# The third step of a graph layer: eight batches' operands stay in SBUF, the bias goes to TensorE, the power moves by a turn

## The chip, the core and the metric

One Trainium2 chip, and of it one core. The metric is the device time of one execution in microseconds; the kernel before has a median of 3002.88 us over three runs (3001.03 to 3012.99).

## The reference, cut to what matters

Four graph layers run over 16 batches of 1024 nodes with 128 features and a dense 0/1 adjacency; each adds its result to its input and normalises. The change is in layer 1, a GraphSAGE of three steps with a batch norm after each:

```python
def _sage(x, adj, Wr, Wx, b, mf):
    deg = jnp.clip(jnp.sum(adj, axis=-1, keepdims=True), 1.0, None)
    agg = jnp.einsum('bij,bjd->bid', adj, x) / deg
    out = agg @ Wr + x @ Wx + b
    nrm = jnp.maximum(jnp.linalg.norm(out, axis=-1, keepdims=True), NORM_EPS)
    return out / nrm * mf[..., None]

h1 = _bn(relu(_sage(x,  adj_d, Wr1, Wx1, b1, mf)), g1, be1)
h2 = _bn(relu(_sage(h1, adj_d, Wr2, Wx2, b2, mf)), g2, be2)
h3 = _bn(relu(_sage(h2, adj_d, Wr3, Wx3, b3, mf)), g3, be3)
out = concat([h1, h2, h3]) @ Wl + bl
```

The batch norm takes mean and variance over all batches and nodes, so no step can begin its products before the step ahead of it has ended its statistics for all 16 batches. The same holds for layer 2, which needs h3.

## The kernel before, in words

`adj_d` is a thinned adjacency that a stage before layer 1 makes. It lies in SBUF as 8-bit numbers, 8 KB per partition and batch: `Y[8]` to `Y[15]` stay where they were made (the left `carry` pool), while `Y[0]` to `Y[7]` are stored to DRAM and loaded again, batch by batch, in steps one and two.

A `Step` has four parts for each batch, each a generator that yields between stages. `load` brings in h transposed (`hT`) and the aggregate (`ag`), 512 KB each, on SP's queue. `out` makes x Wx + agg Wr in two PSUM banks of four node blocks each (L1405), adds the bias row on VectorE (L1407), squares on ScalarE into PSUM (L1413), sums on VectorE (L1414), raises to -1/2 on GpSimd (L743 on VectorE and L744 on GpSimd, inside `power_mhalf`), multiplies by the mask (L1417), and writes n = relu(o) times that factor (L1421). `keep` transposes n (TensorE, L758), copies it to `nT` (ScalarE, L1430), takes the statistics (VectorE, L1431) and stores nT to DRAM from GpSimd's queue (L1432), as the next step and layer 2 read it. In the first two steps `keep` also makes the aggregate for the next step: it splits n in two parts (L1267, L1268), widens the 8-bit adjacency (L1288, L1290), multiplies (L1301), scales by the degree (L1440) and stores `ag` (L1442, GpSimd's queue). The third step has no aggregate to make.

`norm` and `take_norm` close a step: the statistics are combined (L1335), GpSimd raises to -1/2 again, and the batch norm's scale and shift are folded into the next step's weights and bias row (L1328 to L1331).

The order of the turns is written by hand in the loop at the end: all steps go through batches 8 to 15 and then 0 to 7, with loads one or two turns ahead. In the third step a turn holds the first stage of `out` of its batch, the remaining stages of `out` of the batch before, and `keep` of the batch before that. `take_turns` goes round the streams, one stage of each. The order on each engine comes from that source order, and from a planner that moves an instruction forward when it expects the earlier ones to have to wait: the first products of layer 2 (L1563) stand among the last turns of the third step. Each engine executes its own list in order.

Buffers that matter: ps_h and ps_a are two pools of four PSUM banks each. In the third step ps_h serves both the products of `out` and the transposes of `keep`, and ps_a is idle but for the last aggregate of step two. `o` has two buffers, `nT` two, `n`, `ag` and the h of the third step three each.

Of the kernel before, what the change touches and what calls it, by code (L numbers as in the profile page):

```python
# [22 lines left out]
P = 128  # L23
# [616 lines left out]
def fast_kernel(ctx: ExitStack, tc: tile.TileContext, t: dict, out: bass.AP, flag: bass.AP):  # L640
# [612 lines left out]
    with ExitStack() as ph:  # L1253
# [39 lines left out]
        def adjacency_product(pieces, parts):  # L1293

            for h in range(H2):
# [6 lines left out]
                                             start=(jt == 0 and p == 0), stop=(jt == NT - 1 and p == 1))  # L1302
                yield acc, slice(h * 512, (h + 1) * 512)

        class Step:


# [14 lines left out]
            def take_norm(self):  # L1322

                ab = bn_ab[self.l - 1]
                ws = wts.tile([P, P], F32, name="ws")
                nc.vector.tensor_add(ws, self.Wr, self.Wx)
                pc = ps_h.tile([P, P], F32, name="pc", tag="h")
                nc.tensor.matmul(pc, ab[:, 1:2].to_broadcast([P, P]), ws, start=True, stop=True)  # L1328
                nc.vector.tensor_add(self.brow, self.brow, pc)
                nc.vector.tensor_scalar(self.Wr, self.Wr, ab[:, 0:1], None, op0=OP.mult)  # L1330
                nc.vector.tensor_scalar(self.Wx, self.Wx, ab[:, 0:1], None, op0=OP.mult)  # L1331

            def norm(self):
                mv = wts.tile([P, 2], F32, name=f"bmv{self.l}")
# [7 lines left out]
            def load(self, b):  # L1342
                st = self.batches[b]
                if self.l < 2:
                    st.A = Y[b]
                    if b < B // 2:
                        st.A = wide_pool.tile([P, NT, N], FP8, name="A8", bufs=4)
                        nc.sync.dma_start(st.A.bitcast(F32), dil8_d[b])
                if self.l == 0:
                    st.x = work.tile([P, NT, P], F32, name="n", bufs=3)  # L1350
                    nc.sync.dma_start(st.x, nat(x1_d[b]))
                else:

                    tag, bufs = ("rdeg", 3) if self.l == 2 else ("hT", 2)
                    st.hT = work.tile([P, N], F32, name="hT", tag=tag, bufs=bufs)
                    nc.sync.dma_start(st.hT, hT_d[self.l - 1][b])
                    st.ag = work.tile([P, N], F32, name="ag", bufs=3)
                    nc.sync.dma_start(st.ag, ag_d[b])
                    if self.l < 2:
                        self.load_rdeg(b)  # L1360
                yield
# [34 lines left out]
            def out(self, b):  # L1396

                st = self.batches[b]
                o = work.tile([P, NT, P], F32, name="o", tag="oT")
                banks = []  # L1400
                for p, _, blocks in halves(ps_h):
                    banks.append(tiles3(p))
                    for i, j in enumerate(blocks):
                        for n, (x, W) in enumerate(((st.hT, self.Wx), (st.ag, self.Wr))):
                            nc.tensor.matmul(p[:, i * P:(i + 1) * P], x[:, j * P:(j + 1) * P], W,  # L1405
                                             start=(n == 0), stop=(n == 1))
                    nc.vector.tensor_add(o[:, blocks[0]:blocks[-1] + 1, :], tiles3(p),  # L1407
                                         self.brow[:, None, :].to_broadcast([P, 4, P]))
                yield
                ss = small.tile([P, NT], F32, name="ss")  # L1410
                for h, sq in enumerate(banks):
                    k = slice(4 * h, 4 * h + 4)
                    nc.scalar.activation(sq, o[:, k, :], AF.Square)  # L1413
                    nc.vector.tensor_reduce(ss[:, k], sq, AX.X, OP.add)  # L1414
                yield
                rn = power_mhalf(small, ss, floor=1e-24, name="rn")
                nc.vector.tensor_mul(rn, rn, mf[:, b * NT:(b + 1) * NT])  # L1417
                st.n = work.tile([P, NT, P], F32, name="n", bufs=3)
                for h in range(H2):
                    k = slice(4 * h, 4 * h + 4)  # L1420
                    nc.vector.scalar_tensor_tensor(st.n[:, k, :], o[:, k, :], 0.0, half_rows(rn[:, k]),  # L1421
                                                   op0=OP.max, op1=OP.mult)
                yield

            def keep(self, b):

                st = self.batches[b]
                nT = work.tile([P, N], F32, name="nT", tag="hi" if self.l == 2 else "oT")
                for p, c, k in turned(ps_h, st.n):
                    nc.scalar.copy(nT[:, c], p)  # L1430
                    nc.vector.bn_stats(self.stats[:, b * H2 + k.start // 4, :], nT[:, c])  # L1431
# [2 lines left out]
                if self.l < 2:  # L1434
                    parts = split(st.n)
                    pieces = list(widened(st.A))
                    yield
                    ag = work.tile([P, N], F32, name="ag", bufs=3)
                    for acc, c in adjacency_product(pieces, parts):
                        nc.vector.tensor_mul(ag[:, c], acc, st.rdeg[:, c])  # L1440
                        yield
                    nc.gpsimd.dma_start(ag_d[b], ag)  # L1442
                yield

        before = None
# [5 lines left out]
        for l in range(3):  # L1451
            step = Step(l, before)
            if l:
                before.norm()
                step.take_norm()
            lead = 0 if l == 1 else 1
            take_turns([step.load(b) for b in order[:1 + lead]])
            if l == 0:
# [2 lines left out]
            for i in range(B + lag[l]):  # L1461
# [3 lines left out]
                if l == 0 and i + 1 < B:  # L1465
                    streams.append(step.first(order[i + 1]))
                if i < B:
                    streams.append(outs[i] if l < 2 else islice(outs[i], 1))
                if l == 2 and i:
                    streams.append(outs[i - 1])  # L1470
                if i > lag[l]:
# [277 lines left out]
```

## Time and profile before

| what | value |
|---|---|
| median of 3 runs | 3002.88 us (3001.03 to 3012.99) |
| span of the profiled execution, first to last instruction | 2999.4 us |
| PE busy, whole span | 2738.3 us (91%) |
| VectorE (DVE) busy | 2327.9 us (78%) |
| ScalarE (ACT) busy | 2028.5 us (68%) |
| GpSimd (POOL) busy | 324.1 us (11%) |
| mean DMA rate over the span | 99 GB/s |
| layer 1, second step | about 1535 to 1717 us |
| layer 1, third step | 1717.1 us (first product) to 1825.1 us (last statistics) |

The profile comes from a single execution. Its time as a whole is not listed beside the span; the median of the runs is 3.5 us above the span, and that difference is what lies around the first and the last instruction. Busy times are sums of instruction durations with overlapping ones counted once; VectorE's instructions of 128x512 elements last 0.68 us but start every 0.60 us, since each begins before the one ahead of it has drained. PE rows with "x2" show two instructions of one matmul in fp32, which is executed in two passes.

### The profile page before, as it was taken

Reading aid. Unit: us, or ns where it says so; the run is one execution under the profiler, and the core shown is the slowest. Engines: PE = TensorE matmul, PEld = TensorE weight load, DVE = VectorE, ACT = ScalarE, POOL = GpSimd, SP = SyncE. Lnnn points to the kernel's source line nnn. Section 1 sums busy time; section 2 is a strip of 40 time slices with the busy share of each in tenths; the row PEclk is TensorE's granted clock in tenths of the full one; section 3 lists DMA queues with packets and bytes.
Section 4 is the critical chain, followed back from the end, with each engine's and each line's share of the span. In section 5 each row is a group of like instructions: output and inputs, shape, how many; then the busy total and the mean of one; then the engine's idle time right before and its main releaser. Section 6 shows DMA issues by size and latency. Waiting matters only on the chain.

```text
span 2999.4 us, 43064 instructions
## 1 busy us (share of the span) xinstructions
PE 2738.3 (91%) x15282; PEld 1714.8 (57%) x15282; DVE 2327.9 (78%) x5990; ACT 2028.5 (68%) x3476; POOL 324.1 (11%) x295
## 2 busy tenths in 40 slices
PE   7999999996999998999999988999999999999996
PEld 3444444443566566887788874455555555555554
DVE  6898888887999995776688885766767777777765
ACT  5777787784788877666555534766766776666763
POOL 0000000003000001111122231000010001000000
PEclk9999999998999999999999997999999999999998
DMA  4344344431000024223367692111111121111000
GB/s 157 134 162 148 134 147 155 141 134 43 2 2 2 2 82 163 86 99 129 128 238 241 234 342 98 36 57 57 64 70 57 65 70 69 57 56 57 22 15 23
DMA packets 124129, 297.98 MB, mean 99 GB/s; under 512 B 12672, under 2 KB 65664, under 8 KB 116736
## 3 DMA queue, kind: packets, MB, share of 16 engines
q1 hardware_dynamic: 103440, 211.65, 20.8%
q0 software_dynamic: 20464, 83.47, 7.4%
q8 instruction: 123, 2.02, 0.3%
q14 instruction: 102, 0.84, 0.1%
HBM read 211.04 MB, written 84.02 MB: 98 GB/s over the span
## 4 chain that ended last, share of the span: by engine, by line
PE 36%; DVE 23%; issue 21%; ACT 8%; DMA 6%; POOL 5%; SPq 0%; POOLq 0%; ACTq 0%; DVEq 0%
PE ph L1545 8%; PE acc L1301 7%; PE ph L765 4%; PE acc L1621 4%; DMA an<-in_adj 4%; POOL ln_rstd L744 3%; PE pmm L723 3%; DVE ln_st L793 3%; PE ph L1405 3%; ACT xn L800 3%; PE ph L758 3%; DVE em L1607 2%; PE ph L1531 2%; ACT em L969 2%; PE acc L976 2%
## 5 line engine op out<-in xcount | busy, mean ns | idle before, releaser
L723 PE MATMUL pmm<-G,hT 128*128 128x512 f32 x1024 | 503.1, 608 | 7.6 <-DVE mx L1607 7.2
L800 ACT ACTIVATE xn<-xn,ln_nb,ln_rstd 128x128 f32<-128x128 f32 x512 | 207.3, 481 | 108.7 <-DVE ln_nb L798 108.7
L723 PEld LDWEIGHTS pmm<-G,hT 128*128 128x128 f32 x1024 | 178.2, 192 | 175.5 <-issue 140.6
L976 PE MATMUL acc<-em,hs 128*128 128x512 f32 x512 | 243.5, 598 | 16.6 <-DVE hs L973 15.0
L1301 PE MATMUL acc<-a,lo 128*128 128x512 f32 x768 | 243.4, 401 | 15.7 <-DVE lo L1268 15.7
L744 POOL TENSOR_TENSOR ln_rstd<-ln_rstd,mhalf 128x8 f32<-128x8 f32 (+1 forms) x68 | 113.6, 1671 | 1320.0 <-DVE nmx L1609 603.7
L1621 PE MATMUL acc<-em,hs 128*128 128x512 f32 x512 | 249.7, 606 | 3.5 <-DVE hs L1618 1.9
L1301 PE MATMUL acc<-a,hi 128*128 128x512 f32 x768 | 244.0, 402 | 3.7 <-ACT hi L1267 3.5
L1138 PE MATMUL s<-step,carry 128*128 128x512 bf16 (+2 forms) x1088 | 211.6, 307 | 4.1 <-DVE carry L1108 3.2
L1140 ACT ACTIVATE q<-s,negc 128x512 f16<-128x512 f32 x256 | 170.6, 697 | 58.4 <-DVE negc L1119 22.3
L922 ACT ACTIVATE ab<-an 128x1024 bf16<-128x1024 f32 x128 | 134.6, 1053 | 106.2 <-DMA an<-in_adj 79.5
L1152 ACT ACTIVATE carry<-pc,negone 128x512 fp8e4<-128x512 f32 x256 | 166.8, 699 | 37.0 <-PE pc L1151 27.7
L965 DVE CUSTOM_DVE_ANT_0 em<-pmm,msk 128x1024 f32<-128x1024 f32 x128 | 155.9, 1218 | 30.4 <-PE acc L976 26.5
L1607 DVE CUSTOM_DVE_ANT_0 em<-pmm,msk 128x1024 f32<-128x1024 f32 x128 | 155.6, 1216 | 26.1 <-PE acc L1621 21.3
L1301 PEld LDWEIGHTS acc<-a,lo 128*128 128x128 f32 x768 | 144.2, 190 | 54.9 <-DVE lo L1268 21.3
L925 DVE SCALAR_TENSOR_TENSOR chk<-an 128x1024 fp8e4<-128x1024 f32 x128 | 156.3, 1221 | 15.5 <-DMA an<-in_adj 15.4
L1301 PEld LDWEIGHTS acc<-a,hi 128*128 128x128 f32 x768 | 143.0, 190 | 37.1 <-ACT hi L1267 4.0
L1602 ACT ACTIVATE msk<-A,nbig 128x1024 bf16<-128x1024 fp8e4 x128 | 145.8, 1140 | 26.6 <-DVE mx L1607 23.4
L930 DVE TENSOR_SCALAR carry<-pt 128x1024 fp8e4<-128x1024 bf16 x128 | 155.5, 1216 | 7.0 <-PE pt L929 6.9
L976 PEld LDWEIGHTS acc<-em,hs 128*128 128x128 f32 x512 | 90.6, 190 | 113.0 <-issue 87.9
L969 ACT ACTIVATE em<-em,nmx 128x1024 f32<-128x1024 f32 x128 | 146.8, 1147 | 11.9 <-DVE nmx L967 11.5
L1405 PE MATMUL ph<-Wx,hT 128*128 128x128 f32 x768 | 151.6, 280 | 3.0 <-ACT nT L1430 1.5
(293 smaller groups left out, 6252.8 us busy)
## 6 DMA issues: line engine op xcount, KB each, us to landing
an<-in_adj SPq DMA_DIRECT2D x128, 512.0 KB, 4.1
adj_d<-carry POOLq DMA_DIRECT2D x16, 1024.0 KB, 4.9
A<-dil_d SPq DMA_DIRECT2D x16, 1024.0 KB, 6.8
rdeg<-rdeg_d SPq DMA_DIRECT2D x32, 512.0 KB, 4.1
ag_d<-ag POOLq DMA_DIRECT2D x32, 512.0 KB, 5.3
ag<-ag_d SPq DMA_DIRECT2D x32, 512.0 KB, 6.1
A<-adj_d SPq DMA_DIRECT2D x16, 1024.0 KB, 4.7
xn<-in_x SPq DMA_DIRECT2D x16, 512.0 KB, 3.9
```

The lines of the kernel that those rows point to most:

```text
L723: nc.tensor.matmul(p[:, h * 512:(h + 1) * 512], lhsT, rhs[:, h * 512:(h + 1) * 512], start=True, stop=True)
L744: nc.gpsimd.tensor_tensor(r, r, mhalf[:, :n], op=OP.pow)
L800: nc.scalar.activation(r[:, k.start + i, :], r[:, k.start + i, :], AF.Identity, scale=rstd[:, i:i + 1], bias=nb[:, i:i + 1])
L969: nc.scalar.activation(em, em, AF.Exp, bias=nmx, accum_out=sm)
L976: nc.tensor.matmul(s.acc[:, c], hs, em[:, c], start=(jt == 0), stop=(jt == NT - 1))
L1138: nc.tensor.matmul(s[:, lo or 0:], y, twos if lo is None else step[:, :512 - lo], start=(j == 0), stop=(j == len(terms) - 1))
L1140: nc.scalar.activation(q[:, h * 512:(h + 1) * 512], s, AF.Abs, bias=st.negc[:, i:i + 1])
L1301: nc.tensor.matmul(acc, part[:, jt, :], pieces[h * NT // 2 + i][:, j, :], start=(jt == 0 and p == 0), stop=(jt == NT - 1 and p == 1))
L1405: nc.tensor.matmul(p[:, i * P:(i + 1) * P], x[:, j * P:(j + 1) * P], W, start=(n == 0), stop=(n == 1))
L1545: nc.tensor.matmul(p, part[:, jt, :], A[:, jt, c], start=(jt == 0 and i == 0), stop=(jt == NT - 1 and i == 1))
L1607: nc.vector.tensor_tensor_reduce(em, e, msk, 1.0, 0.0, op0=OP.add, op1=OP.max, accum_out=mx)
L1621: nc.tensor.matmul(s.acc[:, c], hs, em[:, c], start=(jt == 0), stop=(jt == NT - 1))
```

## The change

Three parts, all for the third step (`l == 2`).

Where h and the aggregate live. When the second step reaches batch b of 0 to 7, the adjacency `Y[b + 8]` has had its last use eight turns before. `home(b)` takes that memory, 8 KB per partition, as two fp32 rows of 1024: the first becomes nT of batch b, the second its aggregate. The third step's `load` then hands over these two and issues no DMA. nT is still stored to DRAM, because layer 2 reads it; ag of these batches is not. The order of the third step alternates the two kinds of batches: 8, 0, 9, 1, and so on to 15, 7.

The bias. Each bank of the third step's `out` is opened by a bf16 product of 512 columns: a matrix of twos against `bias3`, which holds half the bias row in three bf16 parts in rows 0, 32 and 64 and zeros elsewhere. The products of h and ag accumulate on it. The results stay in PSUM, now in ps_a; the square reads it there and writes `o` in SBUF, and n reads it there. `split_bias` makes the three parts on VectorE at the step's start.

The power. In the third step the second stage of `out` (squares, sums) now also issues the power, and the loop runs two stages of `out` in its batch's own turn; the multiplication by the mask and n come in the turn after.

```diff
--- before.py
+++ after.py
@@ -1302,6 +1302,11 @@
                                              start=(jt == 0 and p == 0), stop=(jt == NT - 1 and p == 1))
                 yield acc, slice(h * 512, (h + 1) * 512)
 
+        def home(b):
+
+            words = Y[b + B // 2].bitcast(F32).rearrange("p t n -> p (t n)")
+            return words[:, :N], words[:, N:]
+
         class Step:
 
 
@@ -1329,6 +1334,21 @@
                 nc.vector.tensor_add(self.brow, self.brow, pc)
                 nc.vector.tensor_scalar(self.Wr, self.Wr, ab[:, 0:1], None, op0=OP.mult)
                 nc.vector.tensor_scalar(self.Wx, self.Wx, ab[:, 0:1], None, op0=OP.mult)
+                if self.l == 2:
+                    self.split_bias()
+
+            def split_bias(self):
+
+                self.bias3 = wts.tile([P, P], BF16, name="bias3")
+                nc.vector.memset(self.bias3, 0.0)
+                rest = wts.tile([P, P], F32, name="ws")
+                nc.vector.tensor_scalar(rest, self.brow, 0.5, None, op0=OP.mult)
+                for i in range(3):
+                    part = wts.tile([P, P], BF16, name="part")
+                    nc.vector.tensor_copy(part, rest)
+                    nc.vector.tensor_copy(self.bias3[32 * i:32 * i + 1, :], part[32 * i:32 * i + 1, :])
+                    if i < 2:
+                        nc.vector.tensor_sub(rest, rest, part)
 
             def norm(self):
                 mv = wts.tile([P, 2], F32, name=f"bmv{self.l}")
@@ -1349,6 +1369,8 @@
                 if self.l == 0:
                     st.x = work.tile([P, NT, P], F32, name="n", bufs=3)
                     nc.sync.dma_start(st.x, nat(x1_d[b]))
+                elif hasattr(st, "home"):
+                    st.hT, st.ag = st.home
                 else:
 
                     tag, bufs = ("rdeg", 3) if self.l == 2 else ("hT", 2)
@@ -1397,35 +1419,48 @@
 
                 st = self.batches[b]
                 o = work.tile([P, NT, P], F32, name="o", tag="oT")
+                end = self.l == 2
                 banks = []
-                for p, _, blocks in halves(ps_h):
+                for p, _, blocks in halves(ps_a, "acc") if end else halves(ps_h):
                     banks.append(tiles3(p))
+                    if end:
+                        nc.tensor.matmul(tiles3(p), twos[:, :P], self.bias3[:, None, :].to_broadcast([P, 4, P]),
+                                         start=True, stop=False)
                     for i, j in enumerate(blocks):
                         for n, (x, W) in enumerate(((st.hT, self.Wx), (st.ag, self.Wr))):
                             nc.tensor.matmul(p[:, i * P:(i + 1) * P], x[:, j * P:(j + 1) * P], W,
-                                             start=(n == 0), stop=(n == 1))
-                    nc.vector.tensor_add(o[:, blocks[0]:blocks[-1] + 1, :], tiles3(p),
-                                         self.brow[:, None, :].to_broadcast([P, 4, P]))
+                                             start=(n == 0 and not end), stop=(n == 1 and (i == 3 or not end)))
+                    if not end:
+                        nc.vector.tensor_add(o[:, blocks[0]:blocks[-1] + 1, :], tiles3(p),
+                                             self.brow[:, None, :].to_broadcast([P, 4, P]))
                 yield
                 ss = small.tile([P, NT], F32, name="ss")
-                for h, sq in enumerate(banks):
+                for h, bank in enumerate(banks):
                     k = slice(4 * h, 4 * h + 4)
-                    nc.scalar.activation(sq, o[:, k, :], AF.Square)
+                    x, sq = (bank, o[:, k, :]) if end else (o[:, k, :], bank)
+                    nc.scalar.activation(sq, x, AF.Square)
                     nc.vector.tensor_reduce(ss[:, k], sq, AX.X, OP.add)
+                if end:
+                    rn = power_mhalf(small, ss, floor=1e-24, name="rn")
                 yield
-                rn = power_mhalf(small, ss, floor=1e-24, name="rn")
+                if not end:
+                    rn = power_mhalf(small, ss, floor=1e-24, name="rn")
                 nc.vector.tensor_mul(rn, rn, mf[:, b * NT:(b + 1) * NT])
                 st.n = work.tile([P, NT, P], F32, name="n", bufs=3)
                 for h in range(H2):
                     k = slice(4 * h, 4 * h + 4)
-                    nc.vector.scalar_tensor_tensor(st.n[:, k, :], o[:, k, :], 0.0, half_rows(rn[:, k]),
+                    nc.vector.scalar_tensor_tensor(st.n[:, k, :], banks[h] if end else o[:, k, :], 0.0, half_rows(rn[:, k]),
                                                    op0=OP.max, op1=OP.mult)
                 yield
 
             def keep(self, b):
 
                 st = self.batches[b]
-                nT = work.tile([P, N], F32, name="nT", tag="hi" if self.l == 2 else "oT")
+                if self.l == 1 and b < B // 2:
+                    st.home = home(b)
+                    nT = st.home[0]
+                else:
+                    nT = work.tile([P, N], F32, name="nT", tag="hi" if self.l == 2 else "oT")
                 for p, c, k in turned(ps_h, st.n):
                     nc.scalar.copy(nT[:, c], p)
                     nc.vector.bn_stats(self.stats[:, b * H2 + k.start // 4, :], nT[:, c])
@@ -1435,11 +1470,13 @@
                     parts = split(st.n)
                     pieces = list(widened(st.A))
                     yield
-                    ag = work.tile([P, N], F32, name="ag", bufs=3)
+                    kept = hasattr(st, "home")
+                    ag = st.home[1] if kept else work.tile([P, N], F32, name="ag", bufs=3)
                     for acc, c in adjacency_product(pieces, parts):
                         nc.vector.tensor_mul(ag[:, c], acc, st.rdeg[:, c])
                         yield
-                    nc.gpsimd.dma_start(ag_d[b], ag)
+                    if not kept:
+                        nc.gpsimd.dma_start(ag_d[b], ag)
                 yield
 
         before = None
@@ -1453,6 +1490,8 @@
             if l:
                 before.norm()
                 step.take_norm()
+            if l == 2:
+                order = [b for pair in zip(order[:B // 2], order[B // 2:]) for b in pair]
             lead = 0 if l == 1 else 1
             take_turns([step.load(b) for b in order[:1 + lead]])
             if l == 0:
@@ -1465,7 +1504,7 @@
                 if l == 0 and i + 1 < B:
                     streams.append(step.first(order[i + 1]))
                 if i < B:
-                    streams.append(outs[i] if l < 2 else islice(outs[i], 1))
+                    streams.append(outs[i] if l < 2 else islice(outs[i], 2))
                 if l == 2 and i:
                     streams.append(outs[i - 1])
                 if i > lag[l]:
```

## The prediction

> **What bounds the kernel now.** I looked first at the busy times of all engines by stretch, to find the third step and its limit. It begins when the new weights are ready (first L1405 of the step at 1717.1 us) and its last statistics end at 1825.1 us: 108 us, 3.6% of the span of 2999.4 us. Nothing that the change touches outside it is late, so this is where it must be priced. Columns: stretch, length, then PE, weight load, DVE, ACT, POOL busy (instructions), granted PE clock, DMA share, GB/s.
>
> ```profile
> 1625.00:1717.00 92.00, 89.95 (x535) 77.70 (x534) 76.63 (x134) 52.64 (x68) 21.24 (x24) 1.00 0.73 251
> 1717.00:1733.00 16.00, 15.43 (x121) 14.51 (x121) 9.85 (x24) 3.43 (x7) 3.12 (x3) 1.00 0.60 186
> 1733.00:1745.00 12.00, 10.06 (x81) 9.21 (x82) 11.05 (x22) 4.22 (x9) 5.09 (x5) 1.00 0.98 354
> 1745.00:1760.00 15.00, 13.94 (x117) 12.85 (x116) 13.78 (x28) 5.61 (x12) 5.11 (x6) 1.00 0.91 310
> 1760.00:1775.00 15.00, 13.73 (x112) 12.47 (x113) 12.99 (x26) 6.52 (x12) 6.20 (x6) 1.00 0.98 382
> 1775.00:1790.00 15.00, 12.56 (x93) 10.36 (x91) 11.77 (x25) 4.29 (x8) 5.25 (x6) 1.00 1.02 388
> 1790.00:1805.00 15.00, 12.16 (x78) 10.22 (x76) 11.48 (x24) 4.28 (x8) 4.79 (x5) 0.89 1.03 379
> 1805.00:1812.00 7.00, 6.91 (x56) 6.08 (x55) 5.67 (x11) 2.20 (x4) 2.31 (x3) 1.00 0.36 142
> 1812.00:1822.00 10.00, 4.28 (x24) 2.47 (x23) 6.95 (x15) 3.19 (x6) 3.99 (x4) 0.91 0.62 212
> 1822.00:1850.00 28.00, 18.91 (x53) 10.70 (x51) 14.11 (x61) 14.37 (x30) 5.20 (x6) 0.56 0.21 75
> ```
>
> The first row is the second step: PE is busy 98% of it, so 4 MB fewer stores there buy nothing. In the third step three resources are nearly full at once: DMA (share 0.91 to 1.03 from 1733 to 1805), DVE (about 90% in the steady part), and PE. From 1717 to 1812 (the last product L1405) PE's busy times add to 84.8 of 95 us. **Only 10.2 us of PE idleness lie in the loop.** That sum decides the forecast.
>
> Next the order of time on DVE, steady part:
>
> ```profile
> 1759.81 1.28 DVE L1407 TENSOR_TENSOR o<-ph,b 128x512 f32<-128x512 f32 x2
> 1761.01 1.27 DVE L1431 BATCH_NORM_STATS2 stats<-nT 128x6 f32<-128x512 f32 x2
> 1762.20 0.15 DVE L743 TENSOR_SCALAR rn<-ss 128x8 f32<-128x8 f32 x1
> 1762.26 0.68 DVE L1414 TENSOR_REDUCE ss<-ph 128x4 f32<-128x512 f32 x1
> 1764.14 0.17 DVE L1417 TENSOR_TENSOR rn<-rn,mf 128x8 f32<-128x8 f32 x1 [1.19 <-POOL rn L744]
> ```
>
> A 128x512 instruction starts every 0.60 us. A turn has eight (L1407, L1414, L1421, L1431, two each), 4.8 us, and small ones; the wait for GpSimd's power adds 1.19 us every second turn. The chain of waits confirms DVE there, and names a store that held a buffer while DMA was full, and a load that PE waited for:
>
> ```profile
> 1733.87 10.22 DMA h2T_d<-nT
> ...
> 1764.30 0.60 DVE ss L1414
> 1764.90 0.61 DVE n L1421
> ...
> 1772.61 7.58 DMA hb<-h1T_d
> ```
>
> Last, PE at the end of the step:
>
> ```profile
> 1812.88 1.02 PE L1563 MATMUL py<-hb,Wl 128*128 128x512 f32 x2
> 1814.28 1.23 PE L758 MATMUL ph<-identf,n 128*128 128x128 f32 x8 [0.38 <-DVE n L1421]
> 1815.35 1.02 PE L1563 MATMUL py<-hb,Wl 128*128 128x512 f32 x2
> 1821.71 1.97 PE L758 MATMUL ph<-identf,n 128*128 128x128 f32 x8 [5.34 <-DVE n L1421]
> ```
>
> From the last L1405 (1812.0) to the end of the statistics it takes 13.1 us, most of it a serial chain through DVE, ACT and POOL; nothing of layer 2's real work can start before.
>
> [...] after 5.34 us of idling the eight transposes take 1.97 us instead of about 1.04, and the clock is 0.56 from 1822 to 1850. [...] in this trace bf16 and fp8 products of 512 columns follow each other in 0.22 to 0.31 us (L1138, L1148 at 902.7 to 903.7). [...]
>
> **The change part by part.**
>
> Bias to TensorE. Removed: 32 L1407 on DVE, 32 x 0.60 = 19.2 us of its issue time, and one link (0.69 us) of each batch's chain. Added: 32 bf16 products of 512 columns on PE. No row shows this operation with this neighbour (the f32 products around it), so bounds: 32 x 0.22 = 7.0 and 32 x 0.31 = 9.9 us; I take 0.25 each, **8.0 us**, on PE and not hidden, since PE will be the fullest engine. DVE falls to 6 x 0.60 + about 0.2 = 3.8 us a turn. PE's turn is 32 L1405 instructions at 0.111 us (3.57), eight transposes (0.88), about 0.1 for the change between them, plus 0.5: 5.05 us. The bound passes from DVE and DMA to PE.
>
> ACT's square now reads PSUM and writes SBUF, the reduction reads SBUF and n reads PSUM: 0.60, 0.68 and 0.68 us today with the sides the other way round, statistics from SBUF 0.68; taken as unchanged, ±0.05 us a turn and under cover of PE.
>
> Banks. A result now stays in one of four ps_a banks until L1421 has read it: two products' halves (4.5) then square 0.6, sum 0.6, L743 0.15, power 1.66 with about 0.25 of hand-over, L1417 0.17, two n 1.2: n is finished some 5.0 us after the batch's last product. PE has 0.88 + 4.5 + 0.88 = 6.3 us of other work before it needs that bank again. Hidden, with 1.3 us to spare; transposes keep ps_h alone, so the waits of L1405 for copies out of ps_h (ACT nT, and l2WT 1.30 at 1795.7) go.
>
> GpSimd a turn ahead. In the source L743 and the power close turn i, L1417 opens the work of turn i+1. Behind L1417 on DVE stand two n, and behind them PE's transposes. The two statistics of an older batch (1.2 us) and PE-paced gaps cover the 1.9 us. The 1.19 us waits go, but they were DVE's, no longer the bound: worth nothing beyond what is counted as idle below.
>
> Memory. For eight batches h, ag loads (16 issues on SP, 8.4 MB) and ag stores (8 on POOL at 0.58 us, 4.2 MB, in step two) go; h is still stored for layer 2. The step moves 300 GB/s x 109 us = 32.7 MB; less 8.4 and about 1 MB of late stores it is some 23 MB, under 260 GB/s in 92 us. DMA is no longer full. The 10.2 us store wait, and at least part of the 2.2 us that PE waited for hb, go. Alternating resident and loaded batches spreads the loads; nothing is added to SP's or POOL's queues. The home was last read eight turns before it is written: no wait.
>
> Split of the bias. DVE gains about ten small instructions after L1329: dependent 128x128 ones take 0.28 + 0.03 us (Wx L1331), six of them 1.9, row copies about 0.3: 2.2 us before the first product of the step can open its bank. 3.4 us of the last adjacency product (L1301, run at 1720.6) are ready to fill PE; if they go first the cost is 0, else 2.2. I take 1.0.
>
> Sum for the loop: busy 84.8, less 1.6 us lost to slow clock at 1796 to 1799 [...], plus 8.0, plus idle that remains, 3 of 10.2 (between 0 and 7): 94.2 against 95.0, **-0.8**. Start **+1.0**. Tail: from last product 0.65 (square), 0.65, 0.2, power 1.9, 0.2, n, transpose, copy, statistics of the last half 3.5: 7.1 against 13.1, **-6.0**, because L1407 no longer queues behind the preceding batch's wait for the power. [...] **-2** (0 to -8). Total -7.8. Against the profiled span that is 2991.6 us; the median of the runs shown, 3002.88, lies 3.5 above the span, so **2995 us**.
>
> **Rivals.** (1) Faster: PE packs tightly. Idle 1, bias 0.22: the loop is 84.8 - 1.6 + 7.0 + 1 = 91.2, -3.8; start 0; tail -6.5; and the clock holds after 1822, where 18.9 us of busy PE at 0.56 hide some 8 us, 6 on the chain: -16, **2987**. For it: DMA and DVE really are relieved. [...] (2) Slower: the power is not ahead. If DVE's queue has L1417 directly after its L743 (as at 1797, 1804, 1818: 1.79 us idle each) or n behind the next batch's sums, banks come back late and PE waits. Today's turn is (95.0 - 3.4 - 5.2 of L1563)/16 = 5.4 us; to lose 15 us over the 6 of the tail it has to be 6.7. Product 4.5, a late chain of 2.2 and no cover is that: 16 x 1.4 - 6 = +16, **3019**. Against: DVE has over 1 us a turn to spare. (3) Nothing comes through: start 2.2, bias 9.9, idle 6, tail -5: about +2, 3005. Layer 2's first work is placed among these turns by a plan made beforehand (L1563 runs at 1775, inside step three), so a new order can move a few us either way in any case.
>
> **How the numbers follow.** 0.5%, 15 us, is about what a measurement of this kernel can tell from no change. Forecast and rival 3 both lie within it: 0.68. Rival 1 and its neighbours beyond 15 us: 0.23. Rival 2: 0.09. The range 2982 to 3009 reaches past rival 1 and rival 3 and leaves out rival 2.
>
> **What would show it.** Right: no L1407 rows in step three, 32 bf16 products of 0.22 to 0.31 us spacing; DMA share under 0.8 from the first turn to the last; PE over 94% busy with turns near 5.1 us; a tail near 7 us. Wrong: idle PE before L1405 released by L1421 (banks), DVE idle 1.8 us before L1417 in most turns, products that wait for bias3 at the start, or a step still near 108 us with DMA full.

## The result, and the profile after

The changed kernel takes 3006.14 us (median of 20 runs), the kernel before 3006.03 us beside it: a ratio of 0.9997, 95% interval 0.9988 to 1.0006. **The time did not change.** The range of the forecast held the value and its likeliest band was right, but the gain of 7.8 us that the sum promised did not arrive.

The two profiled executions can't be compared by their spans, 2999.4 us before and 3009.4 us after: the part ahead of step three, which is the same work but for eight stores, already differs by 5.4 us (the step begins at 1714.22 and 1719.59 us). The later results list a profiled execution's time beside its span, 3011.18 us beside 3009.4 here, so what lies around a span is about 1.8 us and not the 3.5 that the prediction assumed; the profile of before came from an execution at the low end of its runs. So from here on stages are compared. Step three is counted from the instruction that combines step two's statistics (L1335 before, L1355 after) to the one that combines its own.

| step three, us | before | after |
|---|---|---|
| whole step | 110.84 | 113.12 |
| start, to its first product | 2.96 | 6.38 |
| first to last product | 94.60 | 95.51 |
| tail, last product to combined statistics | 13.28 | 11.23 |
| from there to layer 2's first L765 product | 25.61 | 25.35 |

The stretches of the profile after, in the columns of the prediction (stretch, length, PE, weight load, DVE, ACT, POOL busy, granted PE clock, DMA share, GB/s):

```profile
1629.00:1720.00 91.00, 86.62 (x522) 75.64 (x520) 76.37 (x130) 52.88 (x68) 16.88 (x16) 1.00 0.62 219
1720.00:1736.00 16.00, 11.18 (x53) 9.96 (x54) 5.49 (x22) 1.20 (x2) 2.21 (x2) 0.68 0.24 86
...
1766.00:1781.00 15.00, 13.47 (x116) 12.95 (x116) 10.40 (x22) 4.92 (x9) 5.67 (x6) 1.00 1.05 398
1781.00:1796.00 15.00, 12.71 (x108) 12.03 (x107) 10.14 (x21) 5.88 (x11) 6.04 (x6) 1.00 0.52 192
1796.00:1811.00 15.00, 13.69 (x118) 13.17 (x117) 9.81 (x23) 5.54 (x11) 6.17 (x5) 1.00 0.27 107
...
1819.00:1829.00 10.00, 4.96 (x41) 4.30 (x40) 7.40 (x16) 3.33 (x6) 4.47 (x4) 0.89 0.26 106
1829.00:1857.00 28.00, 20.83 (x68) 11.06 (x68) 14.74 (x62) 13.93 (x29) 5.14 (x6) 0.87 0.45 169
```

Of the three full resources DVE went from about 90% to about 68%. DMA is still full from 1766 to 1781 us (1.05), where loads for layer 2 run beside the step's own, and falls to 0.52 and 0.27 after that; the step's last load is issued at 1781.6 us. PE did not fill up in return; in the steady rows it is busy 12.7 to 13.7 us of 15. **When every engine and the DMA have room and the step is no shorter, a chain of waits paces it.** DVE's list in order of time, for one turn, names it (start, duration, instruction, and in brackets the idle time ahead of it and what ended it):

```profile
1768.44 0.16 DVE L743 TENSOR_SCALAR rn<-ss 128x8 f32<-128x8 f32 x1
1770.38 0.17 DVE L1448 TENSOR_TENSOR rn<-rn,mf 128x8 f32<-128x8 f32 x1 [1.79 <-POOL rn L744]
1770.65 1.29 DVE L1452 SCALAR_TENSOR_TENSOR n<-ph,rn 128x512 f32<-128x512 f32 x2
1771.86 1.27 DVE L1442 TENSOR_REDUCE ss<-o 128x4 f32<-128x512 f32 x2
1773.05 1.28 DVE L1466 BATCH_NORM_STATS2 stats<-nT 128x6 f32<-128x512 f32 x2
1774.24 0.15 DVE L743 TENSOR_SCALAR rn<-ss 128x8 f32<-128x8 f32 x1
```

L743 gives GpSimd its operand, and the very next instruction on DVE, L1448, needs GpSimd's result. DVE stands still for 1.79 us. Behind L1448 stand both n, the next batch's sums and an older batch's statistics, so the next L743 is late by all of it: from L743 to L743 it is 1768.44 to 1774.24, **5.80 us in almost every turn**, whether DMA is full or not. Before, turns of 3.82 and 7.45 us alternated in the steady part, 5.63 on average:

```profile
1762.20 0.15 DVE L743 TENSOR_SCALAR rn<-ss 128x8 f32<-128x8 f32 x1
1766.02 0.16 DVE L743 TENSOR_SCALAR rn<-ss 128x8 f32<-128x8 f32 x1
1773.47 0.15 DVE L743 TENSOR_SCALAR rn<-ss 128x8 f32<-128x8 f32 x1
```

After the change the power is a turn ahead in the source and not ahead at all on the engine. The waits of the step, summed (total us, times, longest), say the same, with PE as the next in line, whose bias product waits until n has emptied the bank:

```profile
DVE rn L1448 <- POOL rn L744: 27.0, 16, 1.8
...
PE ph L1427 <- DVE n L1452: 8.5, 12, 0.8
```

In these turns DVE stands still for more than 0.1 us only for GpSimd: neither the sums (L1442) nor the statistics (L1466) wait for a product, a square or a copy. PE and the banks are late because DVE is, and not the other way round. Before, DVE's wait at this place was 15.2 us in all, 11 times. PE in order of time shows the start, two products of the steady part, and the end:

```profile
1722.24 0.76 PE L1333 MATMUL pc<-ws,bn_ab 128*128 128x128 f32 x2 [6.63 <-DVE bn_ab L1360]
1725.59 0.59 PE L1427 MATMUL ph<-bias,step 128*128 128x512 bf16 x1 [2.58 <-DVE bias L1349]
...
1819.70 0.38 PE L1427 MATMUL ph<-bias,step 128*128 128x512 bf16 x1
1819.92 0.38 PE L1431 MATMUL ph<-Wx,carry 128*128 128x128 f32 x2
...
1829.39 1.94 PE L758 MATMUL ph<-identf,n 128*128 128x128 f32 x8 [4.57 <-DVE n L1452]
```

At the start PE idles 6.63 us and 2.58 us more for bias3. Before, it idled 1.06 us there:

```profile
1716.88 0.46 PE L1328 MATMUL pc<-ws,bn_ab 128*128 128x128 f32 x2 [1.06 <-DVE bn_ab L1340]
```

At the end the last transposes still come at half clock after a pause of 4.57 us: the eight take 1.94 us where those at 1821.70 us take 1.04, and the granted clock is 0.50 from 1829 to 1831 us. In between, a bias product costs 0.22 us from its start to the next.

### The profile page after: what moved, and what is told of

It reads as the page before. It is cut to its first block, busy times and chain, and to the rows that moved or that the text cites. A ratio compares the mean times of both kernels' runs of the same rounds, so it can differ in the third digit from the quotient of the medians.

```text
span 3009.4 us, 42956 instructions
## 1 busy us (share of the span) xinstructions
PE 2740.0 (91%) x15251; PEld 1726.5 (57%) x15314; DVE 2312.4 (77%) x5968; ACT 2028.2 (67%) x3476; POOL 319.5 (11%) x287
## 2 busy tenths in 40 slices
DMA packets 120673, 285.39 MB, mean 95 GB/s; under 512 B 12288, under 2 KB 65280, under 8 KB 113280
## 4 chain that ended last, share of the span: by engine, by line
PE 39%; DVE 22%; issue 20%; ACT 9%; DMA 5%; POOL 5%; POOLq 0%; SPq 0%; ACTq 0%; DVEq 0%
PE ph L1584 8%; PE acc L1301 6%; PE ph L765 5%; PE acc L1660 4%; PE ph L1431 4%; DMA an<-in_adj 4%; PE pmm L723 4%; POOL ln_rstd L744 3%; DVE ln_st L793 3%; ACT xn L800 3%; PE ph L758 3%; PE acc L976 2%; PE ph L1570 2%; DVE em L1646 2%; ACT em L969 2%
## 5 line engine op out<-in xcount | busy, mean ns | idle before, releaser
L1138 PE MATMUL s<-step,carry 128*128 128x384 bf16 (+3 forms) x1034 | 198.9, 303 | 7.9 <-DVE carry L1108 3.2
L925 DVE SCALAR_TENSOR_TENSOR chk<-an 128x1024 fp8e4<-128x1024 f32 x128 | 156.3, 1221 | 15.8 <-DMA an<-in_adj 15.2
L962 ACT ACTIVATE msk<-carry,l0nbig 128x1024 bf16<-128x1024 fp8e4 x128 | 142.9, 1139 | 13.9 <-DVE mx L965 8.4
```

What stands on the lines that cost most here:

```text
L1138: nc.tensor.matmul(s[:, lo or 0:], y, twos if lo is None else step[:, :512 - lo], start=(j == 0), stop=(j == len(terms) - 1))
```

## The experiments

Theory A: the step is paced by the exposed power, because L1448 stands directly behind L743. Rivals: B, the banks of ps_a or PE itself; C, DMA; D, a one-time loss at the start. Times are given as ratios to the kernel before, measured beside each one, with 95% intervals; 0.001 is 3 us. The other columns come from one profiled execution each; "turn" is the usual distance from L743 to L743, or between their counterparts, in the steady part.

| kernel | ratio (interval) | step, us | first product | turn | tail |
|---|---|---|---|---|---|
| after | 0.9997 (0.9988 to 1.0006) | 113.12 | 6.38 | 5.80 | 11.23 |
| e1_ahead | 0.9957 (0.9944 to 0.9970) | 100.35 | 6.39 | 4.73 | 8.74 |
| e2_first | 0.9982 (0.9972 to 0.9991) | 106.20 | 8.7 | 5.80 | 11.24 |
| e3_ahead_first | 0.9937 (0.9922 to 0.9951) | 96.82 | 8.87 | 4.74 | 8.74 |
| e4_bias | 1.0005 (0.9997 to 1.0013) | 114.23 | 6.39 | 5.80 | 12.43 |
| e5_nohome | 0.9967 (0.9955 to 0.9979) | 101.17 | 11.40 | 4.74, one 8.77 | 8.74 |
| e6_nobias | 0.9944 (0.9930 to 0.9958) | 90.60 | 5.17 | 4.73 | 9.95 |
| e7_power_only | 1.0021 (1.0010 to 1.0032) | 117.12 | 2.95 | 6.22 | 14.31 |
| e8_home_only | 0.9978 (0.9967 to 0.9989) | 106.25 | 2.96 | 3.83 and 6.3 to 8.2 | 14.00 |
| e9_bias_last | 0.9938 (0.9925 to 0.9951) | 90.87 | 5.16 | 4.74 | 8.97 |
| e10_after_nobias | 0.9983 (0.9976 to 0.9991) | 107.10 | 3.22 | 5.60 | 10.77 |

**e1_ahead: work of an older batch between L743 and the mask.** On the kernel after; `issue_after` is an ordering edge that keeps the statistics behind L743 on the same engine.

```diff
-                    rn = power_mhalf(small, ss, floor=1e-24, name="rn")
+                    rn = small.tile([P, NT], F32, name="rn")
+                    self.floor = nc.vector.tensor_scalar(rn, ss, 1e-24, None, op0=OP.max)
+                    nc.gpsimd.tensor_tensor(rn, rn, mhalf[:, :NT], op=OP.pow)
@@ keep @@
+                late = []
                 for p, c, k in turned(ps_h, st.n):
                     nc.scalar.copy(nT[:, c], p)
-                    nc.vector.bn_stats(self.stats[:, b * H2 + k.start // 4, :], nT[:, c])
+                    late.append((c, k))
+                    if self.l < 2:
+                        nc.vector.bn_stats(self.stats[:, b * H2 + k.start // 4, :], nT[:, c])
                 nc.gpsimd.dma_start(hT_d[self.l][b], nT)
                 yield
+                if self.l == 2:
+                    with tc.issue_after(self.floor.ins):
+                        for c, k in late:
+                            nc.vector.bn_stats(self.stats[:, b * H2 + k.start // 4, :], nT[:, c])
```

> The statistics of the older batch are put between L743 and L1448 on VectorE (order: L743, two statistics, L1448); nothing else differs from the changed kernel. Theory A (the loop is bound by VectorE, which waits 1.79 us for the power in every turn of 5.80 us): 1.2 us of the wait are covered, VectorE needs 4.6 us a turn, PE becomes the bound at 4.95, the turn falls to about 5.0 and the third step by 10 to 12 us (ratio to before about 0.996). Theory B (the four PSUM banks bind: products, square, sums, power and n of one batch must pass before its banks serve again): the order on VectorE does not shorten that chain, the turn stays at 5.8 and the time at that of before. Theory C (DMA still binds): the turn stays at 5.8 too, with the DMA share near 1.0.

It took 0.9957 of the time before, about 12 us less than the kernel after. DVE in order of time:

```profile
1771.19 0.17 DVE L1445 TENSOR_SCALAR rn<-ss 128x8 f32<-128x8 f32 x1
1771.27 1.28 DVE L1477 BATCH_NORM_STATS2 stats<-nT 128x6 f32<-128x512 f32 x2
1773.15 0.17 DVE L1450 TENSOR_TENSOR rn<-rn,mf 128x8 f32<-128x8 f32 x1 [0.60 <-POOL rn L1446]
...
1775.93 0.17 DVE L1445 TENSOR_SCALAR rn<-ss 128x8 f32<-128x8 f32 x1
```

The same instructions in another order: the statistics (L1477) now cover 1.2 of the 1.79 us, 0.60 is left, and the usual turn falls from 5.80 to 4.74 us. Nothing was removed from any engine. This run alone doesn't part A from B: with the statistics gone from between the sums and L743, a bank is free sooner too, which the expectation overlooked. B falls by the list above, where DVE in its turns never waits for PE or a bank, and by e10 below. C falls because the turns of the kernel after are 5.80 us with DMA at 1.05 and at 0.27 alike. With these A is shown.

**e2_first: drain step two's last aggregate ahead of step three.** On the kernel after.

```diff
         for l in range(3):
+            if l == 2:
+                take_turns(left)
+                left = []
             step = Step(l, before)
```

> The last batch's aggregate of step two is written to its end in the source before step three begins; nothing else differs from the changed kernel. Theory D (the start of the step is lost because the 16 products of that aggregate's second half stand behind the first products of the new step, and PE idles 6.6 us for the batch norm and 2.6 us for the split bias): the products fill the 6.6 us, step three is 6 to 7 us shorter, the turns stay at 5.80. Rival: that work has to be done anyway and the wait for the batch norm moves with it (its statistics come later): no gain.

0.9982, some 4.5 us faster than the kernel after (about 4 us to either side), at unchanged turns: D exists beside A. PE in order of time at the start:

```profile
1725.18 0.63 PE L1301 MATMUL acc<-a,lo 128*128 128x512 f32 x2
1725.64 0.38 PE L1333 MATMUL pc<-ws,bn_ab 128*128 128x128 f32 x2
```

L1333 follows a product of the last aggregate with no idle in front of it, where the kernel after had 6.63 us. There, sixteen of these products (about 7.5 us) stood behind the new step's first ones. The first product comes later here (8.7 against 6.4 us), because that work is done ahead of it; the step is 6.9 us shorter.

**e3_ahead_first: both edits.**

> Both edits of the two runs before. Theories A and D add: 16 to 19 us less than the changed kernel and the kernel before, ratio about 0.994. If A fails, about -6; if D fails, about -11; if both, 0.

0.9937, 19 us below the kernel before: in the ratios the two losses add up. In the profile the step is 16.3 us shorter than after, where e1 and e2 were 12.8 and 6.9 us shorter. The stretches in the middle of the step, same columns as above:

```profile
1778.00:1793.00 15.00, 15.00 (x132) 14.78 (x131) 12.48 (x25) 6.73 (x13) 7.43 (x7) 1.00 0.42 169
1793.00:1808.00 15.00, 15.00 (x132) 14.78 (x131) 12.54 (x28) 6.48 (x12) 7.25 (x8) 1.00 0.26 107
```

Now PE is busy 15.00 of 15 us. This is the state that the prediction assumed for the kernel after. PE's own turn, from a batch's first bias product to the next batch's, is 4.87 us here (1760.40 to 1765.27), DVE's usual one 4.74. Earlier in the step two turns are longer, 6.10 and 5.46 us, because the copies to nT wait for a store of h while DMA is full:

```profile
1758.20 1.29 DVE L1477 BATCH_NORM_STATS2 stats<-nT 128x6 f32<-128x512 f32 x2 [1.96 <-ACT nT L1468]
```

**e4_bias: the bias part alone.** The kernel after, with both other parts undone:

```diff
-                if self.l == 1 and b < B // 2:
+                if False:
@@ out @@
-                if end:
-                    rn = power_mhalf(small, ss, floor=1e-24, name="rn")
                 yield
-                if not end:
-                    rn = power_mhalf(small, ss, floor=1e-24, name="rn")
+                rn = power_mhalf(small, ss, floor=1e-24, name="rn")
@@ loop @@
-            if l == 2:
-                order = [b for pair in zip(order[:B // 2], order[B // 2:]) for b in pair]
-                    streams.append(outs[i] if l < 2 else islice(outs[i], 2))
+                    streams.append(outs[i] if l < 2 else islice(outs[i], 1))
```

> Of the three parts only the bias on TensorE, with its banks; h and ag of all batches are stored and loaded as before, the order of batches is that of before, L743 stands where it stood. Theory A: the order on VectorE is the same as in the changed kernel, so the turn is 5.80 and the time equal to the changed kernel within 2 us, the DMA share higher. Rival (the homes carry something that the bias part loses): DMA is full at 5.8 us a turn, stores and loads hold PE as at 1733 and 1780 before, and this kernel is 3 to 8 us slower than the changed one.

1.0005: the power is back in its old place in the source, and the turn is 5.80 us all the same, with L1448's counterpart (L1445) directly behind L743 and the same wait of 1.79 us:

```profile
1766.18 0.15 DVE L743 TENSOR_SCALAR rn<-ss 128x8 f32<-128x8 f32 x1
1768.12 0.17 DVE L1445 TENSOR_TENSOR rn<-rn,mf 128x8 f32<-128x8 f32 x1 [1.79 <-POOL rn L744]
...
1771.98 0.15 DVE L743 TENSOR_SCALAR rn<-ss 128x8 f32<-128x8 f32 x1
```

So the power part does nothing to the turn here: the order on DVE is the same with it and without. The two losses at the start, 6.62 and 2.58 us, are the same too, so they come with the bias part. It moved the step's products into the banks (ps_a) that the last aggregate uses; that this sharing is why the order changed is argued, not shown. The step is nearly as long as after although DMA is full:

```profile
1781.00:1796.00 15.00, 13.47 (x115) 12.95 (x114) 10.55 (x22) 4.92 (x9) 5.66 (x6) 1.00 1.01 361
```

Against the kernel after that is a share of 1.01 for 0.52 and a step longer by 1.1 us. At a turn of 5.80 us no worth of the homes is seen beyond that; the ratios differ by 2.4 us, less than their intervals.

**e5_nohome: e3 without the homes.** The `if False:` and the batch order of e4, on e3.

> The kernel of the run with both edits (statistics between L743 and the mask, last aggregate first), but h and ag of all 16 batches are stored and loaded, and the order of batches is that of before. Theory E (the homes are worth something only when the turn is short): 1.5 MB a turn in 4.74 us is 330 GB/s, and with layer 2's loads DMA is full; some turns grow by 1 to 3 us for a store or a load, the step is 4 to 10 us longer than with homes, ratio to before about 0.996. Rival: DMA never decides, the time equals that of the run with both edits (0.994).

0.9967 against 0.9937: with the order of e3 the homes are worth some 9 us by the runs, with about 6 to either side. In the profiles the step is 4.4 us longer. Of these, 2.5 us lie ahead of the first product: DVE stood still in the middle of splitting the bias, behind an instruction that needs a weight of the last linear layer:

```profile
1727.08 0.23 DVE L1226 COPY shift<-Wl 128x128 f32<-128x128 f32 x1 [2.44 <-DMA Wl<-in_L_gnn_Wl]
```

PE in order of time where it ran dry later:

```profile
1782.93 0.49 PE L1431 MATMUL ph<-Wx,hT 128*128 128x128 f32 x2 [0.98 <-DMA hT<-h1T_d]
1784.53 0.49 PE L1431 MATMUL ph<-Wr,ag 128*128 128x128 f32 x2 [1.11 <-DMA ag<-ag_d]
```

PE waits for h and then for the aggregate, from a DMA at a share of 1.04 and 413 GB/s from 1780 to 1795 us; from 1785.35 to 1788.34 us the products take 0.63 us a pair instead of 0.39 (granted clock 0.89 over the 15 us), and the turn is 8.77 us long. So C costs single turns once A is gone; most of the others stay at 4.74 us.

**e6_nobias and e10_after_nobias: the price of the bias product.** e3 and the kernel after, each without the L1427 product; both leave out the addition of the bias.

```diff
-                    if end:
-                        nc.tensor.matmul(tiles3(p), twos[:, :P], self.bias3[:, None, :].to_broadcast([P, 4, P]),
-                                         start=True, stop=False)
@@
-                                             start=(n == 0 and not end), stop=(n == 1 and (i == 3 or not end)))
+                                             start=(n == 0), stop=(n == 1))
```

> The kernel of the run with both edits, with the 32 bias products left out (the bias is not added; the split is still computed). If PE alone bounds that kernel's turn (4.74 us, PE busy 15.0 of 15 us), the turn falls by 0.43 us, 6 us in all, and the wait of 3.2 us for the split at the step's start goes too: 9 us less, ratio to before about 0.991. If VectorE's chain (L743, power, mask, n, sums, with 0.60 us of wait) is an equal bound, the turn stays at 4.7 and only the 3 us at the start go: 0.993.

> The changed kernel with the 32 bias products left out (the bias is not added; the split is still computed). If PE's bias products are on the changed kernel's path, its turns fall from 5.80 by up to 0.43 us, 6 us in all, and 2.6 us at the start. If VectorE's wait for the power bounds the turn, the turns stay at 5.8 within 0.1 and only the start's 2.6 us go: ratio to before about 0.999.

In the kernel after, the turn goes from 5.80 to 5.60 us and the first product comes 3.2 us earlier (no wait for bias3); the ratio falls from 0.9997 to 0.9983. L1448's counterpart (L1445) still waits 1.79 us behind its L743. Even the 0.20 us a turn come from DVE's order and not from PE: a sum now stands between the mask and n, where 0.27 us passed before n began.

```profile
1766.34 0.17 DVE L1445 TENSOR_TENSOR rn<-rn,mf 128x8 f32<-128x8 f32 x1 [1.79 <-POOL rn L744]
1766.42 0.68 DVE L1439 TENSOR_REDUCE ss<-o 128x4 f32<-128x512 f32 x1
1767.02 1.28 DVE L1449 SCALAR_TENSOR_TENSOR n<-ph,rn 128x512 f32<-128x512 f32 x2
```

So PE is not the pace of the kernel after. On e3 the usual turn stays at 4.73 us without the product, so the loop through L743, GpSimd, n and the sums is a bound of that length by itself, and PE has been filled up to it. The runs show no gain (0.9944 against 0.9937, about 6 us to either side), not even the 3 us expected at the start, though the step of this profile is 6.2 us shorter than e3's. Two turns are 5.45 and 6.33 us here, and the copies to nT wait for stores of h:

```profile
ACT nT L1465 <- DMA h2T_d<-nT: 13.6, 5, 3.8
```

Why the shorter step of the profile isn't in the runs is open.

**e7_power_only: the power part on the kernel before.**

```diff
+                if self.l == 2:
+                    rn = power_mhalf(small, ss, floor=1e-24, name="rn")
                 yield
-                rn = power_mhalf(small, ss, floor=1e-24, name="rn")
+                if self.l < 2:
+                    rn = power_mhalf(small, ss, floor=1e-24, name="rn")
@@ loop @@
-                    streams.append(outs[i] if l < 2 else islice(outs[i], 1))
+                    streams.append(outs[i] if l < 2 else islice(outs[i], 2))
```

> The kernel before with the third part alone: L743 and the power issued in the batch's own turn. Theory A': what counts is the order that VectorE ends up with, and here only one L1407 stands between L743 and the mask, in every turn: wait 1.2 us in every turn instead of every second, turn 8 x 0.60 + 0.3 + 1.2 = 6.2 to 6.3 us against 5.63, the step 6 to 9 us longer, ratio 1.002 to 1.003. Rival (the power really is a turn ahead): no waits before the mask, turn 5.1 to 5.3, some 5 us faster.

1.0021, slower by 6 us. DVE in order of time:

```profile
1766.48 0.16 DVE L743 TENSOR_SCALAR rn<-ss 128x8 f32<-128x8 f32 x1
1766.56 0.68 DVE L1407 TENSOR_TENSOR o<-ph,b 128x512 f32<-128x512 f32 x1
1768.44 0.17 DVE L1420 TENSOR_TENSOR rn<-rn,mf 128x8 f32<-128x8 f32 x1 [1.20 <-POOL rn L744]
```

One bias addition lies between, so 1.20 us is waited, and in nearly every turn instead of every second: issuing the power earlier in the source made DVE's wait more frequent.

**e8_home_only: the homes and the batch order on the kernel before.**

```diff
+                if self.l == 1 and b < B // 2:
+                    st.home = home(b)
+                    nT = st.home[0]
@@ load @@
+                elif hasattr(st, "home"):
+                    st.hT, st.ag = st.home
@@ loop @@
+            if l == 2:
+                order = [b for pair in zip(order[:B // 2], order[B // 2:]) for b in pair]
```

The lines that make the homes and leave out the store of ag are those of the change and are left out here.

> The kernel before with the first part alone: homes for eight batches, alternating order; bias on VectorE, power where it was. VectorE bounds the steady turn at 5.63 and that stays; what goes are the store that held a buffer (about 2 us of PE at 1742) and the load that PE waited for (2 to 4 us): 2 to 5 us faster, ratio 0.9985 to 0.999. Rival: DMA was the real limit of the loop, then 8 to 12 us faster.

0.9978, 6.6 us faster: alone, this part gains. The turns still alternate as before, the short ones at 3.83 us (3.82 before), the long ones between 6.3 and 8.2 (7.45 before), and from 1780 to 1795 us the DMA share is 0.29.

**e9_bias_last: the bias product closes the bank instead of opening it.** On e3.

```diff
-                    if end:
-                        nc.tensor.matmul(tiles3(p), twos[:, :P], self.bias3[:, None, :].to_broadcast([P, 4, P]),
-                                         start=True, stop=False)
                     for i, j in enumerate(blocks):
                         for n, (x, W) in enumerate(((st.hT, self.Wx), (st.ag, self.Wr))):
                             nc.tensor.matmul(p[:, i * P:(i + 1) * P], x[:, j * P:(j + 1) * P], W,
-                                             start=(n == 0 and not end), stop=(n == 1 and (i == 3 or not end)))
+                                             start=(n == 0 and (i == 0 or not end)), stop=(n == 1 and not end))
+                    if end:
+                        nc.tensor.matmul(tiles3(p), twos[:, :P], self.bias3[:, None, :].to_broadcast([P, 4, P]),
+                                         start=False, stop=True)
```

> The kernel with both edits, but each bank's bias product comes after the bank's sixteen f32 products instead of ahead of them. The split of the bias (ready 3.2 us after the weights) is then 1.8 us less in PE's way: step 1.5 to 2 us shorter, ratio to before about 0.993. Rival: that wait was cover for something else (the first loads, the cold clock), no change from 0.9937.

0.9938, median 2991.29 us against 3009.85: faster than both kernels, and not to be told from e3. PE in order of time at the start, where the products of h and ag are L1428 and the bias product is L1431:

```profile
1722.57 0.38 PE L1333 MATMUL pc<-ws,bn_ab 128*128 128x128 f32 x2
...
1726.12 0.38 PE L1431 MATMUL ph<-bias,step 128*128 128x512 bf16 x1 [0.26 <-DVE bias L1349]
```

The wait for bias3 is 0.26 us, where e2 and e3 had 3.17 and 3.16, and it stands behind a bank's products. In the profile the step is 5.9 us shorter than e3's, partly because e3's first products, up to 1734.49 us, took 0.63 us a pair instead of 0.39 after that pause; the runs show no difference, and their intervals, about 4 us to either side each, leave one of most of that size possible. Whether those microseconds are real is open.

## Why the prediction was right and wrong

The value stood by luck: losses at the start and in the loop (+3.4 and +0.9 us) and gains in the tail and after it (−2.1 and −0.3) nearly cancelled, and a gain of 7.8 us would have lain in the same range. The sum was not right.

- **"The two statistics of an older batch (1.2 us) and PE-paced gaps cover the 1.9 us": false, and the step that failed.** It read the order on DVE from the source. The planner put L1448 directly behind its own L743, as rival 2 described. The wait of 1.79 us came every turn and set a turn of 5.80 us; e1, which puts the cover there, shows its worth (turn 4.73 us). Rival 2 was right in its mechanism and too dear in its price: 6.7 us a turn added the late chain to PE's products one after the other, while DVE's loop is 1.94 us from L743 to L1448 plus 3.86 us of issue time, 5.80. (That rule also took 1.4 us for 6.7 less 5.4, which is 1.3.) By the rule a turn of 5.80 against 5.4 us gives 16 x 0.4 - 6 = +0.4 us; that this is about what came is chance, since the tail gained 2.1 us and not 6. Why the planner holds the mask to be ready so soon was not looked into.
- **PE as the next bound, turn 5.05 us: right in kind, 0.2 too long, and not reached.** e3 has PE busy 15.00 of 15 us with a turn of 4.87 us on PE. The bias at 0.25 us was 0.22 (1819.70 to 1819.92 us). 32 of them are 7.0 us, the low end of the bounds.
- **Bank slack 1.3 us: gone.** It took n as finished 5.0 us after the last product, without the wait in DVE's list for an older batch's power. The batch whose last product ends at 1769.8 us has its n finished at 1777.7, 8 us later, and L1427 waited 8.5 us in all.
- **Start +1.0: it was +3.4.** The forecast let 3.4 us of the last aggregate fill PE "if they go first". They did not: about 7.5 us of it went behind. The split of bias3 alone took about the 2.2 us forecast (2.58 of waiting).
- **Tail −6.0: it was −2.1.** The reason given was that nothing queues behind the preceding batch's wait any more. L1407 was gone, but the last batch's sums queued in its place: its last product stood at 1821.48 us, DVE waited for the preceding batch's power until 1822.49, then ran that batch's n, the last batch's sums and two older statistics, and reached the last L743 at 1826.34. In e1 the tail is 8.74 us.
- **Memory: right in size, and without effect on the time.** The whole profile moved 285.39 MB instead of 297.98, the 12.6 forecast. A DMA share under 0.8 in every turn did not come (1.05 from 1766 to 1781 us). The same saving shortened the step by 4.6 us at the old order (e8), 1.1 at a turn of 5.80 (e4, which also undoes the power part), and 4.4 on e3 (e5); by the runs 6.6, 2.4 and 9 us. The intervals of these overlap, so that its worth depends on the turn is likely and not shown.
- **Clock −2: the clock rose, the time did not.** The −2 was the author's estimate; that a shorter pause keeps the clock up was not shown: after 4.57 us of it instead of 5.34 the last eight transposes took 1.94 us instead of 1.97. 1829 to 1857 us shows 0.87 where before had 0.56 (1822 to 1850 us). L1563's work, which moved out of the step, now runs at this place; that it kept the clock up was not tested. Yet layer 2's first L765 product comes 25.35 us after the statistics instead of 25.61.
- **Loop −0.8: +0.9 by the table,** but of other terms: 5.2 us of L1563 left it and about 4 us of the last aggregate (7.5 less the 3.6 of before) entered it. Neither move was in the sum.

The parts measured alone, −6.6 (homes), +6.3 (power) and +1.5 us (bias), nearly cancel as well. That is no account of the kernel after, since the power part changes nothing beside the bias part.

## What to carry to other kernels

Where a planner orders an engine's list, work issued "a turn ahead" in the source is ahead only if other instructions lie between the producer and its consumer on the engine: here 1.79 us were waited with none between and 0.60 with two statistics (e1). Look for that in the order of time, and force it with an ordering edge if it isn't so. A saving on a full resource need not shorten anything while a chain of waits sets the pace: the kernel after moved 12.6 MB less, and its turns were 5.80 us with DMA full and with DMA at a share of 0.27. So remove the chain first and then value the rest. A change made for the steady turns can reorder the hand-over from the step before as well, so look there too.

## What was not expected of the hardware

Loads and stores together reached 398 GB/s (after, 1766 to 1781 us) and 413 GB/s (e5, 1780 to 1795 us) for the core at a DMA share of 1.04 to 1.05, above the 388 of the profile before. The round trip over GpSimd hardly varies: in the turns shown of four kernels it takes 1.94 to 1.96 us from L743's start to the mask multiplication's, for 8 numbers per partition, of which the power itself is 1.66. In the profile before the same instruction takes 0.57 us for one number per partition (1715.51 us), 1.01 for four (1845.16) and 1.66 for eight, so it grows by 0.15 to 0.16 us a number.

No single length of a pause tells here when TensorE's clock falls. In e5 it fell after two pauses of 0.98 and 1.11 us that ended 1.6 us apart (0.63 instead of 0.39 us a pair, as above), and before the change after pauses of 1.38 and 1.30 us that ended 2.1 us apart (1793.62 and 1795.73; the granted clock was 0.50 from 1797 to 1799 us). Ahead of the first bias product a pause of 3.16 us was followed by a low clock in e3, and one of 3.17 us was not in e2 (first line e3, second e2):

```profile
1728.99 0.58 PE L1427 MATMUL ph<-bias,step 128*128 128x512 bf16 x1 [3.16 <-DVE bias L1349]
1729.19 0.38 PE L1427 MATMUL ph<-bias,step 128*128 128x512 bf16 x1 [3.17 <-DVE bias L1349]
```

What decides it is open.
